# Routed experts' weights: fetched per tile from memory, or kept in SBUF and copied

## The chip, the cores and the metric

The kernel runs on one core of a Trainium2 chip. The core's engines work side by side and meet at semaphores: TensorE (PE in the profile; its weight loads are PEld), VectorE (DVE), ScalarE (ACT), GpSimd (POOL) and SyncE (SP), which here only issues transfers. The metric is the time of one execution on the device, in microseconds; lower is better. Times of the kernel are the median over several executions; the profile is of one more.

## The reference, cut to what matters

The whole computes a transformer-like stack on `x` of shape (16, 128, 128): self attention, cross attention, a gated feed-forward, a mixture of experts, an iterative slot attention, and a second mixture of experts. The change is in the two mixtures:

```python
# first mixture, 2048 tokens of width 128, 7 routed experts and a shared one, two experts for each token
h -> sum over the token's top-2 experts e of weight_e * (silu(h @ rg[e].T) * (h @ ru[e].T)) @ rd[e].T  (+ shared)
# rg, ru: (7, 352, 128); rd: (7, 128, 352), float32; width 352 is padded to 384

# second mixture, the same 2048 tokens, 8 experts, one for each token
h -> gate * (relu(h @ W1[e] + b1[e]) @ W2[e] + b2[e])
# W1: (8, 128, 512); W2: (8, 512, 128), float32
```

Which expert a token goes to is found on the chip, so what weights a tile of tokens needs is known only at run time.

## The kernel before

Tokens are sorted by expert into tiles of 128 places, each tile for one expert (some places stay empty). There are 38 tiles in the first mixture (names ending in m) and 23 in the second (names ending in n): the most that can be needed, whatever the routing. The class `Routed` holds the machinery of both, in this order:

- `rows` writes the normalised tokens to a table in device memory (`tok`), from SP's queue.
- `sort` counts places, gives every tile its expert (`row`, then `row_late`, L784 and L846) and every place its token (`frm`, `to`). Then it starts the first weight transfers and the first gathers.
- `weights` (L855) fetches the whole weights of one tile's expert from device memory: SP loads the row number from `row` into a register (`value_load`, L861) and issues one transfer of 576 KB (m) or 578 KB (n) into one of six buffers (`WBUFS`). `tc.issue_after` keeps these transfers in order. `finish` calls it for the tile five further on, once a tile's weights are used up.
- `fetch` (L867) gathers the 128 tokens of a tile from `tok` with an indirect DMA issued by POOL, 12 tiles ahead in m and 6 in n.
- `tiles` (L879) is the loop. For tile j: `up` does the first products into two PSUM banks (`gum`, 2 x 3 blocks of 128x128 in m; `h1n`, 2 x 2 in n); between its halves `turn(j + 1)` transposes the next tile's tokens into the spare quarter of the first bank, and ACT copies them out as `zT`. The activation follows: tanh on ACT and two operations on DVE (`silu_gate`, L950) in m; two halves on ACT and DVE (L1236, L1238) in n. Then `finish(j - 1)` does the down product of the tile before (`ynm`, `ynn`), scales it (`ysm` on ACT, L993, or `ysn` on DVE, L1248 and L1249), and POOL scatters it to device memory with another indirect DMA (`res`, or the output). `ysn` has six buffers.

In m a tile's place weight `wk` (L987) is a small DVE operation on the gathered tokens. After m, `combine` reads the two results of each token back (`ygm`, eight reads of 256 KB from SP's queue) and the slot stage begins. `slot_prologue` prepares the slot stage's products from the constant weights and from the context `ctxn`, loaded after the attention; `cb`, a row per batch, is loaded at the same place and enters the slots' small network through a product with a row of ones (L1170).

The order of instructions on each engine is chosen by a scheduler, which moves independent work forward: parts of `slot_prologue` and of the shared expert (`moe0_shared`) run while `sort` or the tiles wait. Inside `tc.manual_schedule()` the order written down is kept; before the change only the self attention stands in such a block.

Of the kernel before, what the change touches and what calls it, by code (L numbers as in the profile page):

```python
# [19 lines left out]
P = 128  # L20
# [11 lines left out]
WBUFS = 6  # L32
WT = 1156
# [24 lines left out]
def pixart_kernel(  # L58
# [577 lines left out]
    def wide(nm):  # L636
# [3 lines left out]
    wt = ctx.enter_context(tc.tile_pool(name="wt", bufs=WBUFS))  # L640
    rt = ctx.enter_context(tc.tile_pool(name="rt", bufs=1))
    slp = ctx.enter_context(tc.tile_pool(name="slp", bufs=1))
    ctxn = slp.tile([NC, B, D], F32, name="ctxn")
    dma(out=ctxn, in_=ctx_tok.rearrange("b n d -> n b d"))
    cb = slp.tile([P, B, D], F32, name="cb")
    dma(
        out=cb,
        in_=rows[0, R_COND * D : (R_COND + B) * D].partition_broadcast(P).rearrange("p (b d) -> p b d", d=D),
    )


    def glu_body(g, hT):
        u = ph.tile([P, 4, 512], F32, name=f"u{g}", tag="act")
        for c in range(4):
# [6 lines left out]
            V.scalar_tensor_tensor(u[:, c, :], ps[0], col(C_FFB1 + c), ge, ALU.add, ALU.mult)  # L661
        y = psX.tile([P, 4, D], F32, name=f"yg{g}", tag="x")
        token_major(y, lambda c: u[:, c, :], lambda c: gluw[:, 8 + c, :], 4)
# [40 lines left out]
    w_issue = []  # L704

# [5 lines left out]
    class Routed:  # L711


        def __init__(self, nm, ne, nk, w, w0, tok):
            self.nm, self.ne, self.nk, self.w, self.w0, self.tok = nm, ne, nk, w, w0, tok
            self.ws, self.zs, self.st = [], {}, {}
# [40 lines left out]
        def sort(self):  # L757
# [25 lines left out]
            V.tensor_reduce(te, past, AX.X, ALU.add)  # L783
            self.row = self.tile([1, nt], "row", I32)  # L784
            V.tensor_scalar(te, te, float(ne - 1), float(P), ALU.min, ALU.mult)
            V.tensor_scalar(self.row, te, float(self.w0), None, ALU.add)
# [52 lines left out]
            self.row_late = self.tile([1, nt], "row_late", I32)  # L839
            self.ahead = nk * (FETCH - 1)  # L840
            for _ in range(2):
                self.weights()
            for j in range(self.ahead):
                self.fetch(j)
            late = self.frm[:1] if nk == 2 else self.zs[0][:1, :nt].bitcast(I32)
            V.scalar_tensor_tensor(self.row_late, late, 0, self.row, ALU.mult, ALU.add)  # L846
            for _ in range(2, WBUFS - 1):
                self.weights()
# [6 lines left out]
        def weights(self):  # L855
            j = len(self.ws)
            if j == self.nt:
                return
            w = wt.tile([P, WT], F32, name=f"w{self.nm}{j}", tag="w")
            with tc.issue_after(w_issue[-1]) if w_issue else ExitStack():  # L860
                row = nc.sync.value_load(  # L861
                    (self.row if j < 2 else self.row_late)[0:1, j : j + 1], min_val=self.w0, max_val=self.w0 + (self.ne - 1) * P
                )
                w_issue.append(dma(out=w[:, : self.w.shape[1]], in_=self.w[bass.ds(row, P), :]).ins)
            self.ws.append(w)
# [13 lines left out]
        def tiles(self, up, down):  # L879
# [10 lines left out]
            def finish(j):  # L890
                y = ys4[:, 1 + j % 3, :]
                ys = ph.tile([P, D], F32, name=f"ys{self.nm}{j}", tag="ysn", bufs=6)
                down(self.ws[j], acts[j], y, ys, self, j)
                self.weights()
# [7 lines left out]
            ys4 = psX.tile([P, 4, D], F32, name=f"yn{self.nm}", tag="x")  # L902
            turn(0, ys4[:, 0, :])
            for j in range(nt + 1):
                steps = up(self.ws[j], zT[j], f"{self.nm}{j}") if j < nt else None
                if steps:
                    spare = next(steps)
                if j + 1 < nt:
                    turn(j + 1, spare)
                if steps:  # L910
                    acts[j] = next(steps)
                if j >= 1:
                    finish(j - 1)
# [71 lines left out]
    def moe0_down(w, a, y, ys, R, j):  # L985
        wk = rt.tile([P, 1], F32, name=f"wk{j}", tag="wk", bufs=4)
        V.tensor_scalar(wk, R.zs[j][:, D : D + 1], R.sgn[:, j : j + 1], R.sec[:, j : j + 1], ALU.mult, ALU.add)  # L987
        for c in range(3):
            PE.matmul(  # L989
                y, lhsT=a[:, c * P : (c + 1) * P], rhs=w[:, 2 * IP + c * D : 2 * IP + (c + 1) * D],  # L990
                start=(c == 0), stop=(c == 2),
            )
# [398 lines left out]
```

## Time and profile before

| | us |
|---|---|
| median of 3 executions | 924.51 |
| lowest and highest | 924.43 to 932.38 |
| the profiled execution | 933.3 |
| its span (first to last instruction) | 931.4 |

Where the span goes, by the timeline:

| us from the start | what runs |
|---|---|
| 0 to 436 | self and cross attention |
| 436 to 522 | feed-forward, routing, shared experts, sort of m |
| 522 to 543 | gathers start (522.4); rest of the shared experts |
| 543 to 654 | 38 tiles of m; the last scatter ends at 653.7 |
| 655 to 672 | results read back, slot context |
| 672 to 822 | slot iterations |
| 822 to 852 | routing and sort of n |
| 852 to 931 | 23 tiles of n; the last scatter ends at 928.7 |

A line of the page's groups gives the line of the code, engine, operation, what is written from what, shape and count, then the busy time in total, the mean of one in ns, and how long the engine stood idle before it and on whom. A line of the timeline gives start, duration, engine, line, operation, names, shape and count. Some rows that the change touches:

| row | count | mean ns |
|---|---|---|
| tanh of the gate, ACT L953, 128x384 | 38 | 498 |
| the two gate operations, DVE L955 and L956, 128x384 | 38 each | 554 |
| `wk`, DVE L987, 128x1 | 38 | 270 |
| `zT`, ACT L888, 128x128 | 37 | 264 |
| `ysm`, ACT L993, 128x128 | 38 | 367 |
| activations of n, ACT L1236 and DVE L1238, 128x128 | 46 each | 363 and 346 |
| `ysn`, DVE L1248 and L1249, 128x128 | 23 each | 289 and 352 |
| gather and scatter, POOL L874 and L895 (m) | 38 each | 967 and 981 |
| 128x512 copies on ACT, PSUM to SBUF | many | 577 to 590 |

The 61 weight transfers carry 35 MB of the 62 MB that move in all.

### The profile page before, as it was taken

How to read it: one execution, taken by the hardware profiler on the slowest of the kernel's cores; microseconds unless marked ns; L12 is line 12 of the kernel's file. 1: busy time of each engine (PE TensorE's matmuls, PEld its weight loads, DVE VectorE, ACT ScalarE, POOL GpSimd, SP SyncE). 2: the span in 40 equal slices, each digit the busy share in tenths (PEclk: the TensorE clock that was granted, in tenths of full speed). 3: DMA queues.
4: the chain of work that ended last, by engine and by line, in shares of the span. 5: the costliest groups of instructions: out<-in, count | busy, mean ns of one | idle time of the engine just before them, and what ended most of it. 6: DMA issues, size and time to landing. Idle time of an engine off the chain costs nothing.

```text
span 931.4 us, 16297 instructions
## 1 busy us (share of the span) xinstructions
PE 824.5 (89%) x5847; PEld 651.9 (70%) x5847; DVE 592.1 (64%) x1845; ACT 442.2 (47%) x950; POOL 346.4 (37%) x408
## 2 busy tenths in 40 slices
PE   5999999999999999999999687789768989977766
PEld 4588888777778877777665477789446666656655
DVE  4587776669476666668778634445467758864333
ACT  3666676665644444444222022334377667831222
POOL 2233332234232222234421445644343334433554
PEclk9899999999999999999999879999979979975999
DMA  8100000000000000002001437766300000016763
GB/s 313 63 2 1 1 2 2 1 1 1 2 1 1 2 1 2 1 1 71 4 23 60 142 104 227 247 216 207 96 0 1 1 1 1 24 46 205 248 228 104
DMA packets 29563, 61.82 MB, mean 66 GB/s; under 512 B 4266, under 2 KB 18045, under 8 KB 28843
## 3 DMA queue, kind: packets, MB, share of 16 engines
q1 hardware_dynamic: 25211, 51.70, 16.8%
q0 software_dynamic: 4272, 9.09, 3.0%
q8 instruction: 46, 0.75, 0.3%
q14 instruction: 34, 0.28, 0.1%
HBM read 54.01 MB, written 7.23 MB: 66 GB/s over the span
## 4 chain that ended last, share of the span: by engine, by line
PE 66%; DVE 18%; POOL 4%; ACT 4%; issue 4%; another core or an unknown queue 2%; DMA 1%; SPq 0%; POOLq 0%; ACTq 0%; DVEq 0%
PE gum L978 7%; PE po L441 6%; PE pv L339 6%; PE te L431 5%; PE ya L451 5%; PE s L380 4%; PE pk L332 4%; PE s L389 3%; PE ynm L989 3%; PE pq L322 3%; PE h1n L1231 2%; PE ynn L1246 2%; DVE ri L412 2%; PE yg L485 1%
## 5 line engine op out<-in xcount | busy, mean ns | idle before, releaser
L416 POOL TENSOR_TENSOR e<-e,ri 128x1024 f32<-128x1024 f32 (+1 forms) x64 | 100.6, 1573 | 251.9 <-DVE ri L413 208.5
L400 DVE TENSOR_REDUCE mx<-s 128x8 f32<-128x1024 f32 (+1 forms) x64 | 64.4, 1007 | 48.4 <-PE s L389 39.6
L412 DVE TENSOR_REDUCE ri<-e 128x8 f32<-128x1024 f32 (+1 forms) x64 | 64.2, 1003 | 28.4 <-ACT e L408 27.4
L432 ACT COPY eT<-te 128x512 f32<-128x512 f32 (+1 forms) x96 | 56.4, 587 | 51.0 <-PE te L431 50.4
L431 PEld LDWEIGHTS te<-ident,e 128*128 128x128 f32 (+1 forms) x512 | 61.6, 144 | 19.7 <-issue 11.8
L431 PE MATMUL te<-ident,e 128*128 128x128 f32 (+1 forms) x512 | 75.1, 275 | 0.0
L978 PE MATMUL gum<-zTnm,wm 128*128 128x128 f32 x456 | 67.4, 292 | 6.8 <-ACT zTnm L888 6.8
L441 PE MATMUL po<-eT,v 128*64 128x128 f32 (+1 forms) x1024 | 69.4, 277 | 0.0
L322 PE MATMUL pq<-ha,wa 128*128 128x256 f32 x256 | 65.5, 391 | 3.8 <-DVE r L455 2.8
L408 ACT ACTIVATE e<-e 128x1024 f32<-128x1024 f32 (+1 forms) x64 | 57.1, 892 | 23.5 <-DVE e L405 21.7
L978 PEld LDWEIGHTS gum<-zTnm,wm 128*128 128x128 f32 x456 | 61.8, 206 | 8.2 <-ACT zTnm L888 7.5
L441 PEld LDWEIGHTS po<-eT,v 128*64 128x64 f32 (+1 forms) x1024 | 58.0, 137 | 11.8 <-DVE eT L432 6.3
L405 DVE TENSOR_TENSOR e<-s,mx 128x1024 f32<-128x1024 f32 (+1 forms) x64 | 63.8, 997 | 2.0
L451 PEld LDWEIGHTS ya<-wa,oT 128*128 128x128 f32 x512 | 60.8, 192 | 3.9 <-issue 1.4
L451 PE MATMUL ya<-wa,oT 128*128 128x128 f32 x512 | 62.6, 275 | 0.0
L322 PEld LDWEIGHTS pq<-ha,wa 128*128 128x128 f32 x256 | 45.3, 194 | 12.0 <-DVE r L455 4.2
L874 POOL DMA_INDIRECT zsm<-tok,frmm x38 | 36.8, 967 | 41.5 <-DVE secm L852 21.6
L895 POOL DMA_INDIRECT res<-ysm,tom x38 | 37.3, 981 | 37.4 <-ACT ysm L993 20.5
L343 ACT COPY v<-pv 128x512 f32<-128x512 f32 (+1 forms) x64 | 37.3, 585 | 24.1 <-PE pv L339 24.1
L445 ACT COPY oT<-po 128x512 f32<-128x512 f32 x47 | 27.1, 577 | 44.2 <-PE po L441 44.2
L955 DVE SCALAR_TENSOR_TENSOR gsm<-thm,gum 128x384 f32<-128x384 f32 x38 | 21.1, 554 | 35.4 <-ACT thm L953 19.3
L380 PE MATMUL s<-k,ha 128*128 128x308 f32 x128 | 42.6, 436 | 0.0
(388 smaller groups left out, 1881.1 us busy)
## 6 DMA issues: line engine op xcount, KB each, us to landing
wm<-in_moe_w_dram SPq DMA_DIRECT2D x38, 576.0 KB
wn<-in_moe_w_dram SPq DMA_DIRECT2D x23, 578.0 KB
wa<-in_attn_w_dram SPq DMA_DIRECT2D x4, 1024.0 KB
ygm<-res SPq DMA_DIRECT2D x8, 256.0 KB
tok<-stm SPq DMA_DIRECT2D x4, 258.0 KB
tok<-stn SPq DMA_DIRECT2D x4, 258.0 KB
x<-in_x_dram SPq DMA_DIRECT2D x8, 128.0 KB
cb<-in_rows_dram SPq DMA_DIRECT2D x1, 1024.0 KB
```

The costliest lines, as they stand in the source:

```text
L322: PE.matmul(pq[:, j, :], lhsT=wqk[:, w : w + P], rhs=hT, start=True, stop=True)
L380: PE.matmul(ps[:, par, : 4 * nk].rearrange("p (j k) -> p j k", k=nk), lhsT=st["qT"][:, i * P : (i + 1) * P], rhs=st["kT"][:, h0 : h0 + 4, ...
L400: V.tensor_reduce(self.mx, self.ps, AX.X, ALU.max)
L405: V.tensor_tensor(self.e, self.ps, self.mx.unsqueeze(3).to_broadcast([P, 2, 4, nk]), ALU.subtract)
L408: S.activation(self.e, self.e, AF.Exp, scale=1.0 / math.sqrt(DH))
L412: V.tensor_reduce(self.ri, self.e, AX.X, ALU.add)
L416: G.tensor_tensor(self.e, self.e, self.ri.unsqueeze(3).to_broadcast([P, 2, 4, self.nk]), ALU.mult)
L431: PE.transpose(t[:nk, j, :], e[:, par, j, :], ident)
L432: (copies or (S.copy, V.tensor_copy))[par](eT[:nk, par], t[:nk])
L441: PE.matmul(po[par * DH : (par + 1) * DH, j, :], lhsT=st["v"][:nk, i, 8 * hg + 2 * j + par, :], rhs=eT[:nk, par, j, :], start=True, stop=True,
L451: PE.matmul(y, lhsT=oT[:, c, :], rhs=st["wo"][:, 1024 + c * D : 1024 + (c + 1) * D], start=(c == 0), stop=(c == 7),)
L978: PE.matmul(ps[j][:, c * P : (c + 1) * P], lhsT=w[:, k : k + P], rhs=zT, start=True, stop=True)
```

## The change

All routed experts of a mixture are loaded once into one SBUF tile `wall`, in whole experts: `m0.load()` before the feed-forward (7 transfers), `m1.load()` after the tiles of m (8 transfers, into the same tile). For every tile two copies take the expert's part out of it into small buffers, three of each kind: the up part on DVE (128x768 in m, 128x516 in n), the down part on ACT (128x384, 128x640). Their source address is a register of the copying engine; it is loaded by that engine (`address`), right after the copy before. The first three copies of each kind are issued in `sort`, the others in the loop, the up part after a tile's activation, the down part after a tile's down product. `tiles` now stands in a `manual_schedule` block, and `wk` moves from DVE to ACT. The layout of the second mixture's weights puts `b1` behind `W1`. To make room, `ctxn` shares the buffers of `ygm`, the feed-forward's `u` and the shared expert's `ma` share those of the slot stage (`work`), and `cb` keeps four batches on each of four groups of 32 partitions in place of all 16 on every partition.

```diff
-WBUFS = 6
-WT = 1156
+WBUFS = 3
+UP0, DN0 = 768, 384
+UP1, DN1 = 516, 640
...
-    ctxn = slp.tile([NC, B, D], F32, name="ctxn")
-    dma(out=ctxn, in_=ctx_tok.rearrange("b n d -> n b d"))
-    cb = slp.tile([P, B, D], F32, name="cb")
-    dma(
-        out=cb,
-        in_=rows[0, R_COND * D : (R_COND + B) * D].partition_broadcast(P).rearrange("p (b d) -> p b d", d=D),
-    )
+    ctxn = []
+    for g in range(4):
+        ctxn.append(ph.tile([P, 4, D], F32, name=f"ctxn{g}", tag="ygn", bufs=4)[:NC])
+        dma(out=ctxn[g], in_=ctx_tok[4 * g : 4 * g + 4].rearrange("b n d -> n b d"))
+    cb = slp.tile([P, 4, D], F32, name="cb")
+    for g in range(4):
+        k = (R_COND + 4 * g) * D
+        dma(
+            out=cb[32 * g : 32 * g + 32],
+            in_=rows[0, k : k + 4 * D].partition_broadcast(32).rearrange("p (b d) -> p b d", d=D),
+        )
...
+            row = rt.tile([1, NTM], I32, name=f"row0{nm}", tag="row0")[:, :nt]
             self.row = self.tile([1, nt], "row", I32)
-            V.tensor_scalar(te, te, float(ne - 1), float(P), ALU.min, ALU.mult)
-            V.tensor_scalar(self.row, te, float(self.w0), None, ALU.add)
+            V.tensor_scalar(row, te, float(ne - 1), float(self.wn), ALU.min, ALU.mult)
...
-            self.row_late = self.tile([1, nt], "row_late", I32)
             self.ahead = nk * (FETCH - 1)
-            for _ in range(2):
-                self.weights()
             for j in range(self.ahead):
                 self.fetch(j)
-            late = self.frm[:1] if nk == 2 else self.zs[0][:1, :nt].bitcast(I32)
-            V.scalar_tensor_tensor(self.row_late, late, 0, self.row, ALU.mult, ALU.add)
-            for _ in range(2, WBUFS - 1):
-                self.weights()
+            V.scalar_tensor_tensor(self.row, self.frm[:1], 0, row, ALU.mult, ALU.add)
+            for part in range(2):
+                self.address(part)
+                for _ in range(WBUFS):
+                    self.weights(part)
...
-        def weights(self):
-            j = len(self.ws)
+        def load(self):
+
+            self.wall = wt.tile([P, EX1 * (UP1 + DN1)], F32, name=f"wall{self.nm}", tag="wall")
+            for e in range(self.ne):
+                dma(
+                    out=self.wall[:, e * self.wn : (e + 1) * self.wn],
+                    in_=self.w[self.w0 + e * P : self.w0 + (e + 1) * P, :],
+                )
+
+        def address(self, part):
+
+            j = len(self.ws[part])
+            if j < self.nt:
+                self.at[part] = (V, S)[part].value_load(
+                    self.row[0:1, j : j + 1], min_val=0, max_val=(self.ne - 1) * self.wn
+                )
+
+        def weights(self, part):
+
+            j, n = len(self.ws[part]), (self.up, self.dn)[part]
             if j == self.nt:
                 return
-            w = wt.tile([P, WT], F32, name=f"w{self.nm}{j}", tag="w")
-            with tc.issue_after(w_issue[-1]) if w_issue else ExitStack():
-                row = nc.sync.value_load(
-                    (self.row if j < 2 else self.row_late)[0:1, j : j + 1], min_val=self.w0, max_val=self.w0 + (self.ne - 1) * P
-                )
-                w_issue.append(dma(out=w[:, : self.w.shape[1]], in_=self.w[bass.ds(row, P), :]).ins)
-            self.ws.append(w)
+            w = wt.tile([P, (UP0, DN1)[part]], F32, name=f"w{part}{self.nm}{j}", tag=f"w{part}", bufs=WBUFS)[:, :n]
+            (V.tensor_copy, S.copy)[part](w, self.wall[:, bass.ds(self.at[part] + part * self.up, n)])
+            self.ws[part].append(w)
+            self.address(part)
...
-                down(self.ws[j], acts[j], y, ys, self, j)
-                self.weights()
+                down(self.ws[1][j], acts[j], y, ys, self, j)
+                self.weights(1)
...
+            with tc.manual_schedule():
+                ys4 = psX.tile([P, 4, D], F32, name=f"yn{self.nm}", tag="x")
+                turn(0, ys4[:, 0, :])
+                for j in range(nt + 1):
+                    steps = up(self.ws[0][j], zT[j], f"{self.nm}{j}") if j < nt else None
+                    if steps:
+                        spare = next(steps)
+                    if j + 1 < nt:
+                        turn(j + 1, spare)
+                    if steps:
+                        acts[j] = next(steps)
+                        self.weights(0)
+                    if j >= 1:
+                        finish(j - 1)
...
-        V.tensor_scalar(wk, R.zs[j][:, D : D + 1], R.sgn[:, j : j + 1], R.sec[:, j : j + 1], ALU.mult, ALU.add)
+        S.activation(wk, R.zs[j][:, D : D + 1], AF.Identity, bias=R.sec[:, j : j + 1], scale=R.sgn[:, j : j + 1])
...
-        G.tensor_tensor(cb[:1], cb[:1], brow[:1, R_B2S, :].unsqueeze(1).to_broadcast([1, B, D]), ALU.add)
+        row_add(cb, R_B2S, 4)
...
     m0 = Routed("m", EX0 - 1, 2, moe0_w, P, tok0)
     m1 = Routed("n", EX1, 1, moe1_w, 0, tok1)
+    m0.load()
...
     m0.tiles(moe0_up, moe0_down)
+    m1.load()
     slot_prologue()
```

## The prediction

> **What bounds the kernel now.** I read the slices and rates of the page first, then a table of windows, then the two tile loops instruction by instruction, then the chain of waits and the rows that resemble what is added.
>
> The table of windows (us from the start; length, then PE, PEld, DVE, ACT, POOL busy with counts, TensorE clock, DMA share, GB/s):
>
> ```profile
> 522.00:544.00 22.00, 14.84 (x70) 11.40 (x70) 7.94 (x27) 1.35 (x3) 13.50 (x14) 0.73 0.44 150
> 544.00:655.00 111.00, 93.78 (x739) 89.74 (x737) 50.26 (x114) 39.44 (x118) 60.55 (x62) 0.94 0.63 208
> ...
> 861.00:932.00 71.00, 48.69 (x360) 43.68 (x359) 26.50 (x86) 18.48 (x62) 38.13 (x39) 0.96 0.59 194
> ```
>
> Only these two loops (38 tiles "m", 23 tiles "n") and their preludes move much data; the change leaves the attention (0 to 436 us) and the slot stage alone. No engine but PE is near full, and PE is not full in the second. The loops' own limits show in the order of time. A stretch late in the first loop, when the weights had nearly all been fetched:
>
> ```profile
> 632.22 0.83 PE L978 MATMUL gum<-zTnm,wm 128*128 128x128 f32 x6
> 632.28 0.97 POOL L895 DMA_INDIRECT res<-ysm,tom  x1 [1.15 <-ACT ysm L993]
> ...
> 634.34 0.83 PE L978 MATMUL gum<-zTnm,wm 128*128 128x128 f32 x6
> 634.40 0.97 POOL L895 DMA_INDIRECT res<-ysm,tom  x1 [1.15 <-ACT ysm L993]
> ```
>
> One tile every 2.12 us: that is PE's floor for 19 matmul records. But tile 0 starts at 543.3 and the last tile's down product is at 651.1, so the loop takes 108 us, 2.85 per tile. Earlier POOL looks like this:
>
> ```profile
> 569.01 0.98 POOL L895 DMA_INDIRECT res<-ysm,tom  x1 [0.60 <-DVE am L956]
> 570.30 0.99 POOL L874 DMA_INDIRECT zsm<-tok,frmm  x1 [0.30 <-issue]
> 571.59 0.96 POOL L874 DMA_INDIRECT zsm<-tok,frmm  x1 [0.30 <-issue]
> 572.85 1.00 POOL L895 DMA_INDIRECT res<-ysm,tom  x1 [0.30 <-issue]
> ```
>
> A gather or scatter costs POOL 0.97 + 0.30 = 1.27 us, so a tile with both costs 2.54, more than PE's 2.12. And the chain stops every few tiles on something that it cannot name; the 61 weight transfers, whose landings are not recorded, are the likeliest:
>
> ```profile
> 586.73 2.53 another core or an unknown queue
> ...
> 885.13 4.07 another core or an unknown queue
> ```
>
> So today three things share the loops: weight transfers (576 KB a tile, 208 GB/s all told), POOL, and PE.
>
> **The change, part by part.** The sum is against the profiled execution, 933.3 us (span 931.4). That is 1% above the median of 924.51 and near the highest of the three (932.38); I carry the difference over to the median.
>
> *Weights off the path.* 38 x 576 KB and 23 x 578 KB go; 7 and 8 whole experts come (4.0 and 4.6 MB). The first load sits on SP behind `ctxn` and `cb` at 436 us (now eight smaller issues, cb a quarter of its bytes). At the 268 GB/s that one window of the first loop's kind shows it takes 15 us, and SP's next work, the first `tok` write, comes at 466.6: hidden, with about 12 us to spare, else it delays the routing one for one. PE's stops on weights go.
>
> *VectorE's copy.* 128x768 (loop m) or 128x516 (n), fp32, SBUF to SBUF. Nearest rows: `center`, 128x128 with constants, 216 ns, against 289 for the two-input 128x128 of L1248. An element costs 1.0 ns at one per cycle (682 - 554 over 128, L955), and 73 ns less for 128 elements says that `center` went at nearly two per cycle; hence 216 + 640 x 0.52 = 550 ns, and 216 + 388 x 0.52 = 420. At one per cycle it would be 0.9 and 0.7 us. I take the first. DVE's tile is then 0.55 + 0.55 (the gate's two) + 0.55, and 0.27 (`wk`) leaves: 1.65 us, under 2.12.
>
> *ScalarE's copy.* 128x384 or 128x640: from 264 ns (128) and 585 ns (512), 0.84 ns an element, so 0.48 and 0.69. With `wk` (0.27 at most) ACT has 0.50 + 0.26 + 0.37 + 0.27 + 0.48 = 1.88 per m tile.
>
> *Register loads.* One per copy, on DVE and ACT in place of SP. The trace has them on SP only:
>
> ```profile
> 508.34 1.54 SPq L864 DMA_DIRECT2D wm<-in_moe_w_dram  x2
> ...
> 524.32 4.57 SPq L864 DMA_DIRECT2D wm<-in_moe_w_dram  x4
> ```
>
> Two issues end after 1.54, four after 4.57; one issue is 0.37, so a period is 1.17 to 1.40 and load plus address 0.8 to 1.0 us. On DVE and ACT it is zero at the low end, if the running copy and the wait for PE hide it, and 1.0 at the high end, if everything behind it waits; queued behind it are the next tile's gate (DVE) and `zT` and tanh (ACT), and PE's down product waits for those. Half of it exposed: DVE 1.65 + 0.45 = 2.1, ACT 1.88 + 0.45 = 2.3. I take 2.4 per m tile, between this ACT figure and POOL's 2.54 (POOL has only 64 operations in the loop, 12 gathers coming before it: 64 x 1.27 = 81 us, and six `ysn` buffers let PE run ahead). Loop m: 38 x 2.4 = 91, **-17 us**.
>
> Loop n: DVE 0.61 + 0.60 + 0.42 + 0.45 = 2.1, ACT 0.62 + 0.26 + 0.69 + 0.45 = 2.0, POOL (23 + 17) x 1.27 = 51, PE 17 records at 0.11 = 1.9. I take 2.5 per tile: 57.5 plus 5 of filling, against 77 us from the first transpose (851.8) to the last scatter (928.7): **-14 us**.
>
> *The start.* From 522 to 543 `wk` stands in DVE's order behind gathers that have not landed and holds up the shared experts (waits of 1.76 us; the last shared sum waits 6.6 us on an unrecorded event). In the new kernel `wk` is ACT's and inside the hand order. Against it come three copies and loads on each engine right after `frm`: 3 x 1.4 = 4 us on DVE. I take **-5 us** (0 to -10); in loop n, with no such slack, **+1.5**.
>
> *Between the loops.* The second load stands on SP ahead of the eight `ygm` reads. It needs the last copies out of the first `wall`, about three tiles before the end, then 4.6 MB at 268 GB/s = 18 us, so it ends some 11 us after the loop; then the first 0.5 MB of `ygm`. Before, the first combine came 7.5 us after the last scatter (661.2 against 653.7). **+4 us**; at worst +10, if the slot products cannot fill the gap; nothing, if the reads need not queue behind the load.
>
> *The rest.* `wall` costs SBUF, and `work`, `u`, `ma` only change buffers; the `cb` sum goes from 1x2048 (4.5 us on POOL) to 128x512 (1.3), both beside attention's end. Zero; the slot context's reads cover it.
>
> Sum: -17 - 14 - 5 + 1.5 + 4 = -30.5; 933 becomes 903, the median 894.
>
> *A rule that speaks against it.* This trace shows VectorE held while POOL computes:
>
> ```profile
> 440.31 1.27 POOL L248 TENSOR_TENSOR r<-r,brow 128x512 f32<-128x512 f32 x1 [1.97 <-DVE zgl L221]
> 440.40 1.26 DVE L1067 TENSOR_SCALAR gc<-center,cols_sb 128x128 f32<-128x128 f32 x1
> ```
>
> An operation worth 0.28 us lasts until POOL's ends. Four like it beside a gather do not:
>
> ```profile
> 534.88 1.10 DVE L227 TENSOR_SCALAR zc<-ctxn,yc,mvc 77x128 f32<-77x128 f32 x4
> 535.19 0.94 POOL L874 DMA_INDIRECT zsm<-tok,frmm  x1 [0.30 <-issue]
> ```
>
> Both keep their usual length. The Trainium skill, "SBUF — State Buffer", section "Who interferes with whom", says that a VectorE copy using both ports and GpSimd exclude each other for a whole instruction, and that a DMA issued by GpSimd is starved of descriptors meanwhile; this copy is of that kind. By the rule every copy adds its length to POOL: 81 + 38 x 0.55 = 102 us in m and 51 + 23 x 0.42 = 61 in n, so loop m -6, n about -10, and the sum -16 with the other terms. By the row nothing is added. I side with the row, which has only one such meeting.
>
> **Rivals.**
> 1. *The floor.* The loads hide wholly and POOL's lag fits in the buffers: m 81, n 56, start -8: -27 - 21 - 8 + 5 = -51, median 874. For it: the undisturbed 2.12 us stretch. Against: six `ysn` buffers, and ScalarE already waits 22.7 us before `ysm` for something later than the PE it is put down to.
> 2. *POOL locked out by the copies*, or loads fully serial at 0.8 to 1.0: -16 to -8, median 908 to 916.
> 3. *Slower: the register load stalls VectorE.* If a load starts only after the copy, blocks the queue, and is dearer there than on SP, DVE's tile is 1.65 + 0.2 + L. With the other terms, 61 tiles break even at L = 1.1 us; at 1.5 the loops lose 61 x 0.4 = 24 us: median 949. For it: SP already pays 0.8 to 1.0. Against: each load is issued behind a copy that still runs, a tile before its register is used.
> 4. *It does little*, because SP's waits were on free buffers (82 us before L864), not on bandwidth: median 920 to 925.
>
> **How the numbers follow.** About 1% is what a measurement here tells from no change: 915 and 934. My forecast (880 to 912) 0.46, the floor 0.14, rival 2 0.16 (0.06 faster, 0.10 same), slower 0.20, nothing 0.04. So faster 0.66, same 0.14, slower 0.20. The likeliest is 894. The range goes down to 868, just under the floor, and up to 938, taking in rivals 2, 4 and the mild end of 3.
>
> **What would show it.** Right: no large transfer between 522 and the end of loop m; its period 2.1 to 2.5 us; POOL gathers and scatters nearly back to back; a VectorE copy near 0.55. Wrong: a copy of 0.9 or more, gathers stretched beyond 1 us beside copies (the rule), DVE or ACT idle by "issue" for about a us behind each copy (the loads), or a first `ygm` more than 15 us after the last scatter.

## The result, and the profile after

The changed kernel is slower: 951.35 us, median of four executions, against 926.85 of the kernel before beside it; ratio 1.026 (1.020 to 1.031). Forecast were 894 us and at most 938. The profiled execution of the changed kernel took 949.9 us (span 948.2). The profile before is of an execution of 933.3 us, so the stages differ by 16.8 us where the medians differ by 24.5. The spans by stage, cut at the starts of the transposes, scatters and gathers and of the first product on `ygm`:

| | before | after | after less before |
|---|---|---|---|
| first transpose of loop m | 543.3 | 533.1 | -10.2 |
| from it to the last scatter of m | 109.4 | 114.6 | +5.2 |
| from there to the first product on `ygm` | 8.5 | 16.2 | +7.7 |
| from there to the first gather of n | 187.7 | 182.7 | -5.0 |
| from there to the last scatter of n | 78.9 | 97.9 | +19.0 |
| to the end | 3.6 | 3.7 | +0.1 |
| span | 931.4 | 948.2 | +16.8 |

The -5.0 lies in a stage that the change leaves alone; the kernels derived from the changed one took 179 to 192 us there, so it is within the spread of single executions. Windows of the changed kernel's two loops (start:end, length, busy PE, PEld, DVE, ACT, POOL with counts, clock, DMA share, GB/s):

```profile
560.00:620.00 60.00, 48.04 (x373) 43.52 (x374) 31.53 (x59) 32.69 (x99) 39.67 (x39) 1.00 0.15 43
...
846.00:948.00 102.00, 64.61 (x407) 58.74 (x407) 39.03 (x118) 35.61 (x92) 45.83 (x46) 0.82 0.14 41
```

The weights' traffic is gone (43 and 41 GB/s, where the loops of before had about 200), and yet PE still idles: a fifth of loop m, over a third of loop n. No engine is full. So each loop either was not waiting for weights before, or has a new wait now. Loop m is the first case; loop n has a new wait. Loop n in order of time, one tile of 4.0 us:

```profile
892.01 0.29 DVE L1269 TENSOR_TENSOR ysn<-ynn,w1n 128x128 f32<-128x128 f32 x1 [0.34 <-PE h1n L1252]
...
892.38 0.72 ACT L885 COPY w1n<-walln 128x640 f32 x1 [2.04 <-DVE ysn L1269]
...
893.05 0.62 ACT L1257 ACTIVATE an<-h1n,w0n 128x128 f32<-128x128 f32 x2
...
893.73 0.33 PE L908 MATMUL h1n<-ident,zsn 128*128 128x128 f32 x1 [1.90 <-ACT an L1257]
...
894.34 1.06 PE L1267 MATMUL ynn<-w1n,an 128*128 128x128 f32 x8
...
896.02 0.29 DVE L1269 TENSOR_TENSOR ysn<-ynn,w1n 128x128 f32<-128x128 f32 x1 [0.34 <-PE h1n L1252]
...
896.40 0.72 ACT L885 COPY w1n<-walln 128x640 f32 x1 [2.04 <-DVE ysn L1269]
```

Read it as a ring. ScalarE's copy goes into the down buffer that tile j-1 leaves, and the last reader of that buffer is VectorE's `ysn`, which adds b2 out of it (L1269). Behind the copy in ScalarE's order stands the next tile's relu `an`; behind `an` PE's transpose, which writes into the bank that `an` reads; behind the transpose in PE's order the down product; behind that `ysn`, which releases the next copy. What ScalarE waited for between 850 and 940 us (total, times, longest) is one line:

```profile
ACT w1n L885 <- DVE ysn L1269: 43.4, 20, 2.7
```

In loop m, GpSimd in order of time:

```profile
580.20 0.97 POOL L896 DMA_INDIRECT zsm<-tok,frmm  x1 [0.30 <-issue]
581.47 0.99 POOL L917 DMA_INDIRECT res<-ysm,tom  x1 [0.30 <-issue]
582.76 1.20 POOL L896 DMA_INDIRECT zsm<-tok,frmm  x1 [0.30 <-PE ynm L1013]
584.26 0.99 POOL L917 DMA_INDIRECT res<-ysm,tom  x1 [0.30 <-issue]
585.55 0.97 POOL L896 DMA_INDIRECT zsm<-tok,frmm  x1 [0.30 <-issue]
588.22 0.98 POOL L917 DMA_INDIRECT res<-ysm,tom  x1 [1.69 <-ACT ysm L1017]
```

Six operations in 9.3 us, with a pause in each such round: 1.55 us each, although without the pause they would take 1.3. The pause waits for `ysm`. The program lets `ysm` start when PE's down product is done and when the scatter six tiles earlier has given back its buffer (there are six). What ScalarE idled for before `ysm` (total in us, times) is for the most part not named in the changed kernel, and is put down to PE in the kernel before:

```profile
  issue: 23.9, 15
```

```profile
  PE gum L978: 22.7, 9
```

The kernel before has nearly the same pace: its gathers come 3.03 us per tile apart, 1.52 us for each operation, until the last one.

### The profile page after: what moved, and what is told of

The parts are those of the page before. It is cut to its first block, busy times and chain, and to the rows that moved or that the text cites. A ratio compares the mean times of both kernels' runs of the same rounds, so it can differ in the third digit from the quotient of the medians.

```text
span 948.2 us, 16451 instructions
## 1 busy us (share of the span) xinstructions
PE 829.9 (88%) x5847; PEld 653.4 (69%) x5847; DVE 612.9 (65%) x1866; ACT 480.0 (51%) x1047; POOL 348.2 (37%) x408
## 4 chain that ended last, share of the span: by engine, by line
PE 64%; DVE 16%; issue 6%; ACT 5%; POOL 5%; DMA 1%; DVEq 0%; another core or an unknown queue 0%; ACTq 0%; SPq 0%; POOLq 0%
PE po L442 6%; PE pv L340 6%; PE gum L1002 5%; PE te L432 5%; PE ya L452 5%; PE s L381 4%; PE pq L323 4%; PE pk L333 4%; PE s L390 3%; PE ynm L1013 3%; PE glu L667 2%; DVE ri L413 2%; PE ys L1194 1%; PE yg L486 1%; PE gu L989 1%
## 5 line engine op out<-in xcount | busy, mean ns | idle before, releaser
L1002 PE MATMUL gum<-zTnm,w0m 128*128 128x128 f32 x456 | 65.7, 284 | 8.3 <-ACT zTnm L910 8.1
L1002 PEld LDWEIGHTS gum<-zTnm,w0m 128*128 128x128 f32 x456 | 57.7, 194 | 12.6 <-ACT zTnm L910 9.8
L323 PEld LDWEIGHTS pq<-ha,wa 128*128 128x128 f32 x256 | 46.0, 197 | 13.2 <-DVE r L456 4.2
L896 POOL DMA_INDIRECT zsm<-tok,frmm x38 | 39.1, 1030 | 32.5 <-DVE secm L859 21.2
L1013 PE MATMUL ynm<-w1m,am 128*128 128x128 f32 x228 | 34.2, 287 | 11.8 <-ACT ysm L1017 8.4
## 6 DMA issues: line engine op xcount, KB each, us to landing
walln<-in_moe_w_dram SPq DMA_DIRECT2D x8, 578.0 KB, 10.2
```

The source lines that it names most:

```text
L323: PE.matmul(pq[:, j, :], lhsT=wqk[:, w : w + P], rhs=hT, start=True, stop=True)
L1002: PE.matmul(ps[j][:, c * P : (c + 1) * P], lhsT=w[:, k : k + P], rhs=zT, start=True, stop=True)
L1013: PE.matmul(y, lhsT=a[:, c * P : (c + 1) * P], rhs=w[:, c * D : (c + 1) * D], start=(c == 0), stop=(c == 2),)
```

## The experiments

Two theories stood at the start. A: loop n has the ring above, and loop m is held in both kernels by the queue in which the indirect DMAs (GpSimd's gathers and scatters) land, so that taking the weights away freed nothing. B: the copies and register loads themselves fill VectorE and ScalarE. The runs were made on five chips, each beside the kernel before. It took 931.0 us beside e1 to e4 and 927.2 beside e5 to e8, like the chip of the first result: the first kind below. It took 886.7, 886.6 and 888.2 beside e9 to e12, e13 to e16, and e17 and e18: the second kind. Times are compared within a kind alone. e2 to e6, e9, e16 and e17 are single executions; the stages of every run are of one, and e8's is its fastest (924.0). The stages of all:

| | time | pace of m, us per gather and scatter | last scatter of m | from it to first `ygm` product | n, first gather to last scatter |
|---|---|---|---|---|---|
| e1 four down buffers | 941.35 | 3.1 | 652.1 | 15.3 | 80.6 |
| e2 plain gathers in m | 927.0 | 2.12 per tile | 612.9 | 15.3 | 100.2 |
| e3 before, five fetches | 924.66 | 3.0 | 649.5 | 8.4 | 76.4 |
| e4 no copies, no loads | 938.75 | 3.1 | 652.1 | 16.9 | 77.7 |
| e5 12 scatter buffers | 930.38 | 3.1 | 645.8 | 15.2 | 84.7 |
| e6 before, plain gathers in m | 906.85 | 2.12 to 3.4 per tile | 625.0 | 5.3 | 79.8 |
| e7 late load, no hand order | 937.49 | 3.0 | 648.2 | 15.2 | 78.3 |
| e8 late load, late turn | 929.48 | 3.1 | 642.4 | 11.5 | 77.8 |
| e9, e16, e17 half gathers | 915.73, 903.56, 907.06 | 2.7 | 624.2, 620.8, 621.1 | 15.4, 13.2, 13.6 | 76.4, 76.4, 74.7 |
| e10 all mended | 891.57 | 2.8 | 623.8 | 10.5 | 66.0 |
| e11 all but the skip | 891.83 | 2.8 | 623.6 | 10.6 | 64.0 |
| e12 before with the skip | 886.47 | 2.6 | 625.4 | 9.4 | 59.8 |
| e13 the changed kernel again | 925.73 | 2.8 | 621.5 | 13.4 | 98.5 |
| e14 one-port copy | 889.12 | 2.8 | 627.5 | 5.1 | 61.9 |
| e15, e18 two-port copy | 889.58, 888.84 | 2.8 | 623.3, 623.7 | 10.7, 10.7 | 62.2, 62.5 |

**Loop n: the buffer (e1).**

```diff
-tag=f"w{part}", bufs=WBUFS)[:, :n]
+tag=f"w{part}", bufs=WBUFS + part)[:, :n]
```

> The changed kernel with a fourth buffer for the down parts, still copied into the same order and at the same place; nothing else differs. Theory A (a wait that the change added in loop n): ScalarE's copy of tile j+2's down part takes the buffer that tile j-1 has just left, and in loop n VectorE still reads b2 out of that buffer for ysn(j-1); so ScalarE, and behind it the next tile's relu, transpose and first product, wait for ysn each tile (43.4 us of waits in the changed kernel's trace, a period near 4.0 us). With a fourth buffer the copy takes one that is long free: the wait goes, the period falls to about 3.0, loop n shortens by 15 to 22 us and the whole is 930 to 936. Loop m stays as it is (its copy waits for nothing later than the down product): 533 to 649 us, 3.1 us per tile while gathers run. Rival B (the copies' and register loads' own time on VectorE and ScalarE sets the period): 948 to 953, period 4.0. Rival C (the hand order itself, PE's transpose standing behind ScalarE's relu): 945 to 950, a few us at most.

Loop n fell by 17 us, the whole to 941.35, a ratio of 1.0085 (1.0041 to 1.0128) to the kernel before where the changed kernel had 1.026. On the same chip e2, which keeps three buffers in loop n, took 100.2 us there against 80.6. The copy no longer waits for `ysn`; ScalarE's first line is now the ordinary wait for PE:

```profile
ACT an L1257 <- PE h1n L1252: 22.8, 18, 2.2
```

The time itself is a miss against 930 to 936: the expectation counted from 951 with a before of 927, and this chip gave 931. B falls for loop n: the same copies are still made.

**Loop m: the gathers (e2) and, in the kernel before, the gathers (e6) or the weights (e3).** The edit of e2 and e6, in `fetch`; and that of e3, in `weights`:

```diff
-G.indirect_dma_start(out=self.zs[j], ..., ap=self.frm[:, j : j + 1], axis=0)
+dma(out=self.zs[j], in_=self.tok[j % 16 * P : (j % 16 + 1) * P, :])        # loop m only; loop n as before
```

```diff
+if j >= WBUFS - 1:
+    self.ws.append(self.ws[j % (WBUFS - 1)])
+    return
```

> The changed kernel with the 38 gathers of loop m replaced by plain reads of fixed rows of tok issued by SP (the routed rows of loop m are then not the right ones); scatters stay on GpSimd, loop n is untouched. Theory A (the queue of indirect DMAs holds loop m): while each tile has a gather and a scatter, these two move at about 1.55 us each, and ysm waits for a free buffer, that is for a scatter issued six tiles earlier; without the gathers the whole loop goes at 2.1 to 2.3 us per tile, loop m takes 82 to 92 instead of 116 us, and the whole is 920 to 928. Rival B (copies, register loads and wk on VectorE and ScalarE hold the tile at 3.1 us): loop m 112 to 117, whole 946 to 953. Rival C (only GpSimd's own 2.54 us for two issues counts): also 82 to 92, and then GpSimd in the changed kernel ought to be busy back to back, which its 13.2 of 20 us speaks against.

> The kernel before with weights fetched only for the first five tiles of each loop and used again by all later ones (so later tiles work with other experts' weights); gathers, scatters and order as before, and neither copies nor register loads. The step of the prediction (weight transfers hold PE in both loops): loop m falls from 110 to about 93 us and loop n from 77 to about 63, the whole is about 893 to 900. Theory A (the indirect DMA queue holds loop m, so that fetches cost nothing there): loop m 106 to 111 with 3.0 us per tile while gathers run, and only loop n gains, 5 to 12 us from its stops of 3.4 to 4.1 us that no view could name: whole 912 to 920. If fetches cost nothing in either: 922 to 928.

> The kernel before with the 38 gathers of loop m replaced by plain reads of fixed rows of tok issued by SP, among its weight fetches (the routed rows are then not the right ones); everything else as it was. Theory A (the indirect DMA queue also held the kernel before in loop m, not the weights): loop m falls from 110 us to 84 to 94 and the whole to 900 to 912, with all 38 weight fetches still made. The step of the prediction (weight transfers of 576 KB a tile hold it at 2.8 us per tile, 208 GB/s): loop m stays at 104 to 112 and the whole at 920 to 930. A cross with SP's queue, where reads of rows now stand behind weights that wait for a buffer, could leave it between: 94 to 104.

With all copies, register loads and scatters in place, e2 runs loop m at PE's floor, here a window of 60 us without idle time on PE:

```profile
540.00:600.00 60.00, 60.00 (x540) 60.00 (x539) 44.56 (x85) 47.94 (x142) 34.20 (x29) 1.00 0.19 57
```

In the kernel before, taking away all weight transfers but ten (e3) left loop m at 107.9 us and loop n at 76.4, against 109.4 and 78.9 in the profile before; taking away its indirect gathers and leaving the 38 transfers of loop m (e6) left loop m at 91. That is the reverse of the forecast's step. In e6 the first 17 tiles go at 2.12 us, the next at 2.3 to 3.4, where row reads stand among weight issues in SP's queue; that these cause it was not tested.

**What kind of limit (e4, e5).** e4 lets the products read a fixed expert in the store and drops copies and loads; e5 has four down buffers and `bufs=12` for the scatters' sources.

> The changed kernel without copies and register loads: the products read a fixed expert's part of the SBUF store for each tile (not the routed one); the hand order, wk on ScalarE and the loads of whole experts stay. It shows what the copies and the waits that they bring cost. Theory A: loop m as in the changed kernel while gathers run (3.0 to 3.1 us per tile, 108 to 116 us in all), loop n without its wait, 2.6 to 3.0 us per tile, 20 to 28 us shorter; whole 920 to 930. Rival B (the engines' time for copies sets both loops): loop m 85 to 95, loop n 60 to 65 from its first transpose, whole 890 to 905. Rival C (the hand order sets both): whole 940 or more, period of n near 4.

> The changed kernel with four down buffers, as in the run before, and with 12 instead of six buffers for the scatters' sources (ysm, ysn). It tells what kind of limit the indirect DMA queue is in loop m, where ysm waits about 2.0 us every third tile for the landing of a scatter six tiles back. Theory A1 (the queue has a rate: a gather or scatter of 64 KB takes about 1.55 us in it): the pace while gathers run stays near 3.1 us per tile, the last gather is issued at 618 to 626 us, as with six buffers; the waits only move to another place (gathered rows arrive late). Theory A2 (a fixed delay between issue and landing, with too few buffers to cover it): the pace falls to GpSimd's 2.54 us per tile, the last gather is issued at 600 to 608 us and loop m ends 8 to 12 us earlier. Whole: A1 938 to 942, A2 928 to 933.

e4: loop m keeps its 3.1 us, loop n is within 3 us of e1, so the copies cost little beyond the ring. e5: with twice the buffers the pace stays 3.1 us and the last gather is issued at 621.1. So the pace is not a lack of buffers. But it is not a full queue either, for the rows move on both kinds of chips alike. The queue's packets (packets, MB, share of the DMA engines' time) in the changed kernel on the first kind, and on the second (e13):

```profile
q0 software_dynamic: 4272, 9.09, 3.3%
```

```profile
q0 software_dynamic: 4272, 9.09, 3.4%
```

Taken in order, while gathers run, the last packet of a gather or scatter starts 1.7 to 2.6 us after GpSimd began to issue it in the changed kernel, and 1.7 to 2.9 in e13; even beside the weights, in the kernel before, it is at most 5.1. The scatter of six tiles earlier was issued 16 to 18 us before, so its rows had long moved when `ysm` waited. What the waits end on differs. On the second kind it is the scatter's buffer, as the profile says for e13:

```profile
  DMA res<-ysm,tom: 12.7, 10
```

On the first kind the traces point to PE. While gathers run, each of the 16 waits over 0.5 us before `ysm` in the changed kernel ended within 0.1 us of a signal of PE's semaphore (e5: 16 of 16; the kernel before: 15 of 16); three of the 16 were as near to a signal of an indirect DMA. And PE's signals come late there. Between 545 and 605 us, 17 of the 64 in the trace of the changed kernel, and 33 of 72 before, lie within 0.05 us of the end that the profile gives to a product; in e13 all 102 do, and all 102 in e2, which has no indirect gathers in this loop. So what holds loop m on the first kind comes with its indirect gathers, as e2 and e6 show. That it reaches `ysm` through PE's signals is the likelier reading, and not shown: the trace of the changed kernel lacks 16 of those 80 signals and over half of the indirect DMAs', so a scatter's signal that came late is not excluded, and the ends of products are modelled. Why gathers delay anything on these chips and not on the others stays open.

**Mending the other two places (e7, e8, e10, e11).** All have four down buffers. e7 and e8 moved `m1.load()` behind `slot_turns` in the program; e7 also dropped `manual_schedule` (the hand order), e8 kept it and made `moe1_up` hand out its spare quarter after both halves, so that the transpose no longer stands behind the relu. e10 and e11 add to e8 an explicit order between the issues, and e10 also skips the padding places of loop m in its scatters, as e12 does in the kernel before:

```diff
-dma(out=y, in_=res0[n : n + 4 * P, :]...)
+self.read = dma(out=y, in_=res0[n : n + 4 * P, :]...).ins
...
+with tc.issue_after(m0.read):                                # each of the eight loads for n
...
-in_=ys, in_offset=None, **({} if self.nk == 2 else dict(bounds_check=NTOK - 1, oob_is_err=False)),
+in_=ys, in_offset=None, bounds_check=self.nk * NTOK - 1, oob_is_err=False,     # e10, e12
```

> The changed kernel with four down buffers, with the second load of whole experts issued behind the ygm reads instead of ahead of them, and without the hand order in both tile loops. Three places are read one by one. Between the loops: the first product on ygm came 16.2 us after the last scatter in the changed kernel (15.3 with four buffers) and 8.5 in the kernel before; with the load behind, 8 to 9 (if the load ahead was the cause), else 15. Loop n, first gather to end: 101.6 us in the changed kernel, 84.3 with four buffers, 82.5 before; without the hand order 76 to 82 if PE's transpose standing behind ScalarE's relu (0.9 us of PE per tile) held it, 83 to 86 if the queue of gathers and scatters holds it. Loop m: 3.1 us per tile while gathers run, as before, if the queue holds it (its end 647 to 653 us); worse by up to 10 if the hand order was needed against waits on late rows. Whole: 926 to 934.

> The changed kernel with four down buffers, with the second load issued behind the ygm reads, and with the hand order kept but PE's transpose of the next tile in loop n moved behind the second half of the up products (it then no longer stands behind ScalarE's relu). Between the loops 8 to 9 us instead of 15 to 16. Loop n, first gather to end: 72 to 78 us if the hand order held it at 2.9 us per tile (PE's own 1.95 to 2.2 then show after the last gather), 82 to 85 if the gathers and scatters hold it at 1.5 us each. Loop m as with four buffers. Whole: 924 to 930, or 930 to 934 in the second case.

> The version that the runs so far point to: four down buffers; the second load of experts held behind the last ygm read by an order between the two issues (without it the scheduler had put the load ahead again); PE's transpose in loop n behind the second half of the up products; and in loop m the scatters skip the padding slots (768 of 4864 rows, which are written to spare rows that nothing reads), as loop n's already do. Theory A-rows: the queue is relieved of 16% of loop m's scatter rows, 25 of them beside gathers: 25 x 20 rows x 12 ns = 6 us off loop m. Between the loops 8.5 to 9.5 us instead of 11.5 to 15. Loop n 80 to 82 from first gather to end. Whole 914 to 922, 0.985 to 0.995 of the kernel before. If skipped rows cost the queue as much as written ones: 920 to 926.

> The same without the skipping of padding slots in loop m. Between the loops 8.5 to 9.5 us; the rest as with the late turn. Whole 920 to 926, 0.992 to 1.0 of the kernel before; loop m from the first gather to the last one 98 to 101 us.

> The kernel before with nothing changed but that loop m's scatters skip the padding slots. Theory A-rows: its loop m, too, is held by the indirect queue and shortens by 4 to 7 us, whole 920 to 923. The step of the prediction (weight transfers hold it), or a queue that pays for skipped rows as well: 925 to 928, no change.

In e7 and e8 the load was not late, so they missed the 8 to 9 us expected between the loops: written behind, it was put ahead again by the scheduler in large part (six and five of the eight transfers), and the gap stayed 15.2 and 11.5 us. SP's queue in e8, and then in e10 with the order:

```profile
636.89 2.64 SPq L866 DMA_DIRECT2D walln<-in_moe_w_dram  x5
648.09 2.03 SPq L949 DMA_DIRECT2D ygm<-res  x4
650.16 1.06 SPq L866 DMA_DIRECT2D walln<-in_moe_w_dram  x2
```

```profile
626.12 14.36 SPq L950 DMA_DIRECT2D ygm<-res  x8
640.58 4.74 SPq L867 DMA_DIRECT2D walln<-in_moe_w_dram  x8
```

The gap is 10.5 us in e10, 13.4 in the changed kernel on a like chip (e13), and 9.4 in e12. On the first kind the hand order shows no clear cost in loop n: 77.7, 80.6 and 84.7 us with it (e4, e1, e5), 78.3 without (e7), 77.8 with the late transpose (e8).

The skipping of padding did nothing: e10 and e11 are equal, and e12 stands at 0.999 (0.996 to 1.001). But this tells nothing of the first kind, for on this chip the pauses are not there. GpSimd in e12, in order of time:

```profile
592.55 0.99 POOL L874 DMA_INDIRECT zsm<-tok,frmm  x1 [0.30 <-PE gum L978]
593.85 0.97 POOL L874 DMA_INDIRECT zsm<-tok,frmm  x1 [0.30 <-issue]
595.12 1.02 POOL L895 DMA_INDIRECT res<-ysm,tom  x1 [0.31 <-ACT ysm L993]
596.45 1.00 POOL L895 DMA_INDIRECT res<-ysm,tom  x1 [0.30 <-DMA res<-ysm,tom]
597.75 0.99 POOL L874 DMA_INDIRECT zsm<-tok,frmm  x1 [0.30 <-PE gum L978]
```

1.30 us each, GpSimd's own pace. And with the pauses gone, the first 21 tiles of that kernel show what weights cost loop m, at 299 GB/s:

```profile
541.00:585.00 44.00, 44.00 (x395) 43.88 (x395) 26.87 (x61) 20.84 (x62) 32.96 (x34) 1.00 0.89 299
```

Nothing: PE does not idle. The difference between the two kinds of chips (931.4 against 884.5 in the spans of before and e12) is the two loops: m's last scatter comes 27 us earlier, and n is 19 us shorter.

**The changed kernel where GpSimd is the limit (e13), and the half gathers (e9, e16, e17).** In the half gathers GpSimd gathers 64 rows of a tile of loop m and SP reads the other 64 as a plain block; they have four down buffers.

> The changed kernel as it is, beside the kernel before on this chip. If the indirect queue is the limit here (before near 927): 945 to 955, ratio 1.02 to 1.03, loop m 3.1 us per tile while gathers run, loop n 4.0. If GpSimd's issue is the limit (before near 887): loop n still about 4.0 us per tile, since that wait is a chain between ScalarE, PE and VectorE and not of the queue, so 20 to 30 us worse than before there; between the loops 15 to 16 us; loop m ends at the same time as before's within 3 us. Whole 915 to 925, ratio 1.03 to 1.04.

> The changed kernel with four down buffers; in loop m each gather takes 64 rows instead of 128, and SP reads the other 64 rows of the tile as one plain block of tok (those rows are not the routed ones). The number of GpSimd's instructions stays, the rows in the indirect queue fall from 256 to 192 per tile. Theory A-rows (the queue's rate is in rows, about 12 ns each, 1.55 us for 128): while gathers run a tile takes 192 x 12 ns = 2.3 to 2.4 us instead of 3.1, the last gather is issued at 602 to 608 us, loop m ends at 632 to 640. Theory A-instructions (about 1.55 us per gather or scatter, whatever its size): 3.1 us per tile, last gather at 620 to 625, end at 647 to 652. A fall of GpSimd's own time per gather below 0.97 us would show that it, too, goes by rows.

> The kernel with half of each gather's rows read plainly by SP once more (those 64 rows of a tile are not the routed ones), on this chip. If the indirect queue is the limit here (3.1 us per tile with whole gathers): A-rows 2.3 to 2.5 us per tile and the last gather issued at 602 to 610 us; A-instructions 3.1 us and 620 to 625. If GpSimd's issue is the limit: 2.7 us per tile as with whole gathers, and it does not tell.

> Half of each gather's rows of loop m read plainly by SP, as twice before (those 64 rows of a tile are not the routed ones). If before takes about 927 here: A-rows 2.3 to 2.5 us per tile while gathers run and the last gather issued at 602 to 610 us; A-instructions 3.1 us and 620 to 625. If before takes about 887: 2.7 us per tile, which tells nothing.

Here the change costs more, 1.042 (1.037 to 1.047): loop n takes 98.5 us against 59.8 in e12, since the kernel before is faster there and the ring is not. e16, with the fourth buffer, is at 76.4 and 2.9 us per tile; e15, with the hand order in m only, at 62.2; e13, e15 and e16 ran on one chip. So on these chips the ring costs 22 us and the rest of the hand order another 14. Most of the 14 is the transpose behind the relu: with the hand order kept and the transpose late, e10 and e11 are at 66.0 and 64.0. On the first kind this wait shows on PE in e1, though not in the time of loop n:

```profile
910.76 0.33 PE L908 MATMUL h1n<-ident,zsn 128*128 128x128 f32 x1 [0.96 <-ACT an L1257]
```

Whether the pace on the first kind goes by rows or by instructions stays open: the half gathers ran on the second kind alone.

**The copy's form (e14, e15, e18).** All three have four down buffers, the ordered second load and the hand order in loop m alone. Instead of `V.tensor_copy(w, src)`, e14 has `V.scalar_tensor_tensor(w, src, 0.0, src, ALU.mult, ALU.add)`.

> Four down buffers, the second load held behind the ygm reads, the hand order in loop m only, and VectorE's copy of the up part written as an operation with two inputs (x times 0 plus x, the same values), which goes at one element per cycle: 0.9 to 1.0 us for 128x768 instead of 0.55, 0.68 for 128x516. The rule (a VectorE copy that uses both ports keeps GpSimd's DMA from being issued): GpSimd's gathers and scatters in loop m fall from a mean of 1.03 to 1.06 us to 0.97 to 0.98, and where GpSimd is the limit loop m shortens by 3 to 6 us against the next run. The other theory (the stretch comes from more traffic, not from the ports): mean stays above 1.02. Where the indirect queue is the limit the time moves by less than 3 us either way, with the same means.

> The same kernel as the run before with VectorE's plain copy: 0.55 us for 128x768; GpSimd's gathers and scatters at a mean of 1.03 to 1.06 us in loop m. Against the version with the hand order in both loops and the late turn: loop n equal where the queue is the limit, 3 to 5 us shorter where GpSimd is (a tile at 2.2 us instead of 2.45).

> Four down buffers, the second load behind the ygm reads, the hand order in loop m only, once more. If before takes about 927 here (the queue is the limit): between the loops 8.5 to 9.5 us, loop n 80 to 82 us, loop m ending 2 to 6 us before that of the kernel before: 918 to 926, ratio 0.99 to 1.0. If before takes about 887: ratio 1.002 to 1.006 as before.

The means of loop m's scatters (count, busy us, mean ns) in the changed kernel, in e4 without copies, and in e14:

```profile
L917 POOL DMA_INDIRECT res<-ysm,tom x38 | 39.0, 1028 | 36.9 <-ACT ysm L1017 30.2 <-issue 4.8 <-ACT wk L1011 1.0
```

```profile
L915 POOL DMA_INDIRECT res<-ysm,tom x38 | 37.3, 982 | 44.5 <-ACT ysm L1015 20.1 <-ACT zTnm L908 17.8 <-issue 5.0
```

```profile
L922 POOL DMA_INDIRECT res<-ysm,tom x38 | 41.5, 1091 | 11.6 <-issue 2.4 <-DMA res<-ysm,tom 2.1 <-ACT ysm L1022 1.5
```

The copies do stretch GpSimd's DMAs: by about 0.05 us each in the mean of the changed kernel, and by 0.2 in e2, whose scatters took 1180 ns beside a copy in every tile at PE's floor, against 964 in e6 with plain gathers and no copies. But the slower form (0.954 us a copy) stretches them more, not less (1091 ns against 1054 in e15), and the two kernels take the same time. e14's form reads SBUF twice, so it does not show which port it is.

No version beat the kernel before. The best, e18, stands at 0.9998 (0.9977 to 1.0019) of it, the same kernel as e15 at 1.0043 (1.0022 to 1.0064) on another chip. Neither this version nor e10 ran on a chip of the first kind.

## Why the prediction was wrong

- *Loop m, -17.* Failed at its first term, "PE's stops on weights go". The stops that it gave to the weights were not theirs: without the weights the loop kept its 3.0 us per tile (e3), and beside 299 GB/s of them PE did not idle (e12). They came with the indirect gathers: without these, loop m took 83 us with all copies and loads in place (e2). So the sums of VectorE and ScalarE were not the error. The second error is beside the first: "a gather or scatter costs POOL 0.97 + 0.30" leaves out the pauses, and on this chip one came every 1.55 us. The trace before had the sign of it: 1.52 us per operation, and `ysm` waiting for something later than PE's product, which rival 1 names as an objection and does not price. Rival 4, given 0.04, was right that the transfers were not what PE waited for. On the second kind the changed loop m does take the forecast's 91 us (91.6 in e13), by luck: the kernel before takes 86.4 there (e12).
- *Loop n, -14.* Failed at "DVE 2.1, ACT 2.0": sums per engine. The added copy was never followed to the buffer that it fills, whose last reader here is `ysn`, nor to what stands behind it on ScalarE. The cost was +19 us; e1 returns 17 of it.
- *Start, -5.* The first transpose came 10 us earlier, but the gathers set the pace of loop m from the first on, so its end gained only 5 us. The reason given does not suffice: e4 and e7 also have `wk` on ScalarE, e4 inside the hand order, and start at 541. What does bring the early start was not settled.
- *Between the loops, +4.* The mechanism was right. The first product on `ygm` came 7.7 us later, but in the changed kernel PE spent the wait on the slot context's products, and those were then done; from the last scatter to the first gather of n it is 196.2 us before and 198.9 after. On the second kind it is 195.7 before (e12), 201.3 in e13 and 197.2 with the load held back (e10, e15), so the load costs about 4 us there, as forecast, as far as single executions show. Windows of the changed kernel show the load fill the transfers (the last three columns are clock, DMA share and GB/s). The `ygm` reads are issued at 653.3, 5.6 us after the last scatter against 2.4 before, and the first lands at 658.2, as the load ends:

```profile
650.00:655.00 5.00, 3.99 (x13) 2.84 (x14) 0.22 (x1) 1.98 (x4) 0.00 (x0) 0.50 1.03 416
655.00:660.00 5.00, 4.88 (x24) 3.36 (x23) 2.22 (x9) 1.89 (x4) 0.00 (x0) 0.83 0.94 309
```

- *Copies and register loads.* The copies' durations held: 0.55 to 0.60 us and 0.50 on m, 0.43 and 0.72 on n. A register load alone took 0.30 us on VectorE and 0.28 on ScalarE (medians); with its address it had been put at 0.8 to 1.0. Half of each load was to be exposed; e2 shows none of it, at 2.12 us per tile. Rival 3, a stalled VectorE, has the right sign with the wrong mechanism.
- *The first load, nothing.* This held: the first gather of m starts at 522.3 us, against 522.4 before.
- *The rule on ports.* I sided with a row against it, and both ends were off: a stretch exists, but it is 0.05 us in this kernel and 0.2 in e2, where the rule was to add 0.55. So the exclusion for a whole instruction that the Trainium skill, "SBUF — State Buffer", section "Who interferes with whom", states of such a copy shows here as no more than part of one; that the stretch comes from this port is neither borne out (e14) nor excluded.

## What to carry to other kernels

Before a copy is put into a hand-written order, write down which instruction reads its destination last and what stands behind the copy on its engine; the sum of an engine's durations shows neither. Take the pace of a loop's indirect DMAs from how often they come in the trace (1.52 us), not from the length of one (1.27), and find out what fills the difference before anything else is removed. And before a transfer is removed, starve it in a cheap run (five fetches, used again): that run took 924.66 us beside 930.95, so it would have shown how little there was to gain.

## What the runs showed of the hardware

Beside indirect gathers, one kind of chip pauses and the other does not: GpSimd's gathers and scatters of loop m come 1.52 to 1.55 us apart where the kernel before takes 927 to 931 us, and 1.30 where it takes 887 (e12). Their rows move within 1.7 to 2.9 us of the issue on both (changed kernel, e13); what comes late on the first kind are PE's signals, as far as its traces show. The pauses and a shorter loop n make the 40 us between the chips, and they change the verdict on a change: 1.026 on the one kind, 1.042 on the other. Each chip was measured at one time only, so a cause that lies in the time and not in the chip is not excluded. GpSimd's time for a gather hardly depends on its rows: 986 ns for 64 rows (e16), 1031 for 128 (e13), means of the 31 gathers within the loop.
